# The integers of a quantized hidden layer: which are made beside the attention, where their ring of buffers lies, and which engine scales them

## The chip, the cores and the metric

The kernel runs on one core of one Trainium2 chip. The metric is the device time in microseconds of the whole program on that core; a number is the median of several executions. Beside it there is one profiled execution, whose trace gives every instruction's start and duration on each engine: TensorE (PE, matrix multiplication), VectorE (DVE), ScalarE (ACT), GpSimd (POOL), and SyncE (SP), which here only issues transfers. Transfers between the device memory (HBM) and the on-chip memory (SBUF) run on the core's 16 DMA engines, whichever engine issues them.

## The reference, cut to what matters

Two "Flamingo" layers work on x of shape (2, 2048, 512), 4096 rows of 512. Each layer is a gated cross attention to 128 context rows, then a gated feed-forward part. Everything up to the second layer's cross attention is the same before and after the change. The second feed-forward part is the place of the change:

```
x = x + tanh(g_xattn[1]) * xattn(layernorm(x), ctx)          # 16 heads of 64
h = bit_linear(layernorm(x), w1)                             # 512 -> 2048
h = silu(depthwise_conv1d(h) over the 2048 rows of a batch)  # three taps
x = x + tanh(g_ffn[1]) * bit_linear(h, w2)                   # 2048 -> 512
bit_linear(x, w): act_quant(x) times weight_quant(w)
act_quant(x): scale = 127 / max|x| of the row;  round(x * scale) / scale
weight_quant(w): scale = 1 / mean|w|;  clip(round(w * scale), -1, 1) / scale
```

The scale of a row of h is known only when all 2048 hidden values of that row have been computed. Then every value is multiplied by its row's scale and rounded to an integer, and the integers, which fit bf16 exactly, are multiplied with the ternary w2.

## The kernel before, in words

**Blocks.** Rows go in 8 blocks of 512 (4 for each batch). A block's hidden layer is held transposed: hidden units on the 128 partitions, 16 chunks (`HC`) of 128 units, 512 rows along the free dimension. So a block's hidden layer is 128 x 16 x 512, 4 MB in f32 and 2 MB as bf16 integers.

**Beside the attention (lines 213 to 328 and 1022 to 1124).** `cross_attention` runs 128 units, 16 for each block, plus 12 that let the pipeline run out. After a block's output projection (`back`, L315), `stage3_done` stores the block's rows to `x3_d` and queues two generators in `stream`: `quantize_rows` (layer norm and integers of the rows) and `first_half` (the matmuls L1002 with w1, the convolution L1012 to L1018, silu L1043, a store of the f32 hidden layer to `h_d` at L1049, the absolute maximum L1050 to L1056). When a block's first half is over, `scales_of` (queued in `ending`) makes its rows' scales (L1073, `hid_s`). After each unit, `beside4` moves these generators on.

For the first `EARLY` blocks (4 of them) a third list, `later`, holds `integers(g)`: chunk by chunk it loads `h_d` (L1094, `hf`, two buffers), multiplies by the scale on DVE (L1101), rounds (even chunks on DVE, L1107; odd ones with two ACT instructions, L1104 and L1105) and stores the bf16 integers to `hq_d` (L1108). `beside4` moves `later` on by one chunk in three of four units.

**The second half (from line 1271).** For each of the 8 blocks in turn, four row tiles (`down_and_out`): 16 matmuls each (L1232) of the block's integers `hq` with w2, then DVE adds the result to the row tile (L1235) and SP stores it (L1236). Row tiles are loaded from `x3_d` one block ahead (`row_tile`, L1162), into a ring of 8 (`x5`), the first ones into a ring of two (`x5w`). A ninth group of 32 matmuls (`ql`) does the last row of each batch. The integers come from `quantize_hidden(g)`, one block ahead: for `g < EARLY` it only loads `hq_d` (L1198); for the others it loads the f32 hidden layer in 8 pieces of two chunks (L1188, issued by ACT, `h5`), multiplies by the scale (L1207: three pieces of four on DVE, the fourth on POOL), and rounds (even pieces on DVE, L1215; odd ones with two ACT instructions, L1212 and L1213). The last block's hidden layer stays in SBUF. Blocks 6 and 7 finish their first halves inside this second half, beside the matmuls of blocks 0 to 3.

**Where buffers lie.** Pool `w5` takes the memory of the attention's working tiles, which is free as soon as the last unit is done (`second_half_starts`). Pool `act5` takes the memory of the attention's weights, which is free only after the last output projection. Before the change, even blocks' integers lie in `w5` (8 tiles) and odd blocks' in `act5` (8 tiles), and the `h5` pieces lie in both (2 and 4).

**Order.** Each engine's instruction order is fixed when the program is built: a scheduler in the framework merges the generators' instructions into one order for each engine, and each engine executes its own in that order, waiting on semaphores. Transfers take one of eight semaphores in turn, SP's and ACT's together, and the build makes each transfer wait until the one eight before it has landed.

Of the kernel before, what the change touches and what calls it, by code (L numbers as in the profile page):

```python
# [10 lines left out]
F32 = mybir.dt.float32  # L11
BF16 = mybir.dt.bfloat16
# [5 lines left out]
P = 128  # L18
B, S, D = 2, 2048, 512
NT = B * S // P  # L20
TPB = S // P
BLK = 512
TB = BLK // P
NBLK = S // BLK
# [8 lines left out]
HC = HID // P  # L33
# [10 lines left out]
def flamingo_kernel(ctx: ExitStack, tc: tile.TileContext, a: dict, out: bass.AP):  # L44
    nc = tc.nc
# [4 lines left out]
    def psum_pool(stack, name, bufs):  # L50
        return stack.enter_context(tc.tile_pool(name=name, bufs=bufs, space=PSUM))
# [875 lines left out]
    hid_f = const.tile([P, NT], F32, name="hid_f")  # L927
    h_d = [dramp.tile([P, HC, BLK], F32, name=f"h_d{g}") for g in range(B * NBLK)]
    LAST = B * NBLK - 1
    EARLY = 4  # L930
    hq_d = [dramp.tile([P, HC, BLK], BF16, name=f"hq_d{g}") for g in range(EARLY)]
    x3_d = [dramp.tile([S, D], F32, name=f"x3_d{b}") for b in range(B)]

# [61 lines left out]
    carry, ending, kept, act5 = {}, [], [], []  # L995
# [71 lines left out]
    def scales_of(g, amax):  # L1067
# [9 lines left out]
        nc.vector.tensor_scalar(hid_f[:, ts(g, TB)], inv, finstep, None, ALU.mult)  # L1077
        if g < EARLY:
            later.append(integers(g))

    def scales_spread(g):

        pb = ps_mm.tile([P, BLK], F32, name="pb5", tag="mm")
        bcast_rows(pb, hid_s[:, ts(g, TB)], ident)
        s_b = act4.tile([P, BLK], F32, name="s_b", tag="s_b", bufs=1)
        nc.scalar.copy(s_b, pb)
        return s_b

    def integers(g):


        def load(c):
            h = act4.tile([P, BLK], F32, name="hf", tag="hf", bufs=2)
            nc.sync.dma_start(out=h, in_=h_d[g][:, c, :])  # L1094
            return h

        s_b, h = scales_spread(g), load(0)
        for c in range(HC):
            behind = load(c + 1) if c + 1 < HC else None
            yield  # L1100
            nc.vector.tensor_tensor(h, h, s_b, ALU.mult)  # L1101
            q = act4.tile([P, BLK], BF16, name="hi", tag="hi", bufs=2)
            if c % 2:
                nc.scalar.activation(h, h, AF.Copy, bias=RND)  # L1104
                nc.scalar.activation(q, h, AF.Copy, bias=-RND)  # L1105
            else:
                nc.vector.tensor_scalar(q, h, RND, RND, ALU.add, ALU.subtract)  # L1107
            nc.sync.dma_start(out=hq_d[g][:, c, :], in_=q)  # L1108
            h = behind

    stream, later = [], []

    def advance(q):
        while q and next(q[0], q) is q:
            q.pop(0)

    def beside4(u, share=2):


        for _ in range(share):  # L1120
            advance(ending)
            advance(stream)
        if u is None or u % 4 != 1:
            advance(later)

    def stage3_done(n, tiles):
        for i, t in enumerate(tiles):
# [20 lines left out]


    w5, ps_5, quantizing, ahead = [], [], [], []  # L1150
    GQ, hq, used = 2, {}, []

    def row_tile(g, i):

        t = w5[0].tile([P, D], F32, name="x5w", tag="x5w", bufs=2)
        if g + i > 1:
            t = act5[0].tile([P, D], F32, name="x5", tag="x5", bufs=8)
        r, p = g % NBLK * BLK + i * P - 1, 0
        if r < 0:
            nc.sync.dma_start(out=t[0:1, :], in_=x3_d[g // NBLK][0:1, :])  # L1160
            r, p = 0, 1
        nc.sync.dma_start(out=t[p:, :], in_=x3_d[g // NBLK][ds(r, P - p), :])  # L1162
        return t, r, p

    def second_half_starts():
        units.close()
        w5.append(s4.enter_context(tc.tile_pool(name="w5", bufs=1)))
        w5.append(w5[0].tile([P, HC, D], BF16, name="w2q"))
        quantizing.append(quantize_hidden(0))
        nc.sync.dma_start(out=w5[1], in_=w2_d)  # L1170
        ps_5.append(psum_pool(s4, "s5_o", 4))
        next(quantizing[0], None)
        ahead.extend(row_tile(0, i) for i in range(2))

    def quantize_hidden(g):

        NK = HC // GQ
        hq[g] = []

        def load(k):  # L1180
            if g == LAST:
                return kept[k * GQ // GC][:, ds(k * GQ % GC, GQ), :]
            pool = (act5 if len(used) % 3 else w5)[0]
            used.append(g)
            h = pool.tile(
                [P, GQ, BLK], F32, name="h5", tag="h5", bufs=4 if pool is act5[0] else 2
            )
            nc.scalar.dma_start(out=h, in_=h_d[g][:, ts(k, GQ), :])  # L1188
            return h

        def integer_tile():
            pool = act5[0] if g % 2 else w5[0]
            hq[g].append(pool.tile([P, GQ, BLK], BF16, name="hq", tag="hq", bufs=NK))
            return hq[g][-1]

        if g < EARLY:
            for k in range(NK):
                nc.sync.dma_start(out=integer_tile(), in_=hq_d[g][:, ts(k, GQ), :])  # L1198
            return
        AHEAD = 4  # L1200
        hs = [load(k) for k in range(AHEAD)]
        s_b = scales_spread(g)
        yield
        for k in range(NK):
            h = hs.pop(0)
            eng = nc.gpsimd if k % 4 == 3 else nc.vector
            eng.tensor_tensor(  # L1207
                h, h, s_b.unsqueeze(1).to_broadcast([P, GQ, BLK]), ALU.mult
            )
            q = integer_tile()  # L1210
            if k % 2:
                nc.scalar.activation(h, h, AF.Copy, bias=RND)  # L1212
                nc.scalar.activation(q, h, AF.Copy, bias=-RND)  # L1213
            else:
                nc.vector.tensor_scalar(q, h, RND, RND, ALU.add, ALU.subtract)  # L1215
            if k + AHEAD < NK:
                hs.append(load(k + AHEAD))
            yield
# [19 lines left out]
    def last_tokens():  # L1238

        h = act5[0].tile([P, B, HC], F32, name="hl", tag="hl")  # L1240
        nc.scalar.activation(h, z_last, AF.Silu)
        own = row4.tile([P, B], F32, name="ownl", tag="lm")
        nc.vector.tensor_reduce(own, h, AX.X, ALU.max, apply_absolute_value=True)
        pm = ps_mm.tile([P, B, P], F32, name="pml", tag="mm")
        for b in range(B):
            nc.tensor.transpose(pm[:, b, :], own[:, b : b + 1].to_broadcast([P, P]), ident)
        m = row4.tile([P, B], F32, name="ml", tag="lm")
        nc.vector.tensor_reduce(m, pm, AX.X, ALU.max)
        nc.vector.tensor_scalar(m, m, 1e-5, None, ALU.max)
        s = row4.tile([P, B], F32, name="sl", tag="ls")  # L1250
        nc.vector.reciprocal(s, m)
        nc.vector.tensor_scalar(s, s, 127.0, None, ALU.mult)
        fin = row4.tile([P, B], F32, name="fl", tag="lf")
        nc.vector.reciprocal(fin, s)
        nc.vector.tensor_scalar(fin, fin, finstep, None, ALU.mult)
        q = act5[0].tile([P, B, HC], BF16, name="ql", tag="ql")
        for b in range(B):
            nc.vector.tensor_scalar(h[:, b, :], h[:, b, :], s[:, b : b + 1], None, ALU.mult)
        nc.vector.tensor_scalar(q, h, RND, RND, ALU.add, ALU.subtract)
        for b in range(B):  # L1260
            t = act5[0].tile([P, D], F32, name="x5", tag="x5", bufs=8)[0:1, :]
            nc.sync.dma_start(out=t, in_=x3_d[b][S - 1 : S, :])
            down_and_out(
                lambda c: q[:, b, c : c + 1],
                fin[0:1, b : b + 1],
                1,
                t,
                out[(b + 1) * S - 1 : (b + 1) * S, :],
            )

    while later:
        advance(later)
    ahead.extend(row_tile(0, i) for i in range(2, TB))
    for g in range(LAST + 1):
        if g == LAST - 1:
            while stream or ending:
                beside4(None)
            last_tokens()
        behind = quantize_hidden(g + 1) if g < LAST else iter(())
        for i in range(TB):  # L1280
            t, r, p = ahead.pop(0)
            down_and_out(
                lambda c: hq[g][c // GQ][:, c % GQ, ts(i, P)],
                hid_f[:, g * TB + i : g * TB + i + 1],
                P,
                t,
                out[ds(g // NBLK * S + r, P - p), :],
                p,
            )
            if g < LAST:  # L1290
                ahead.append(row_tile(g + 1, i))
            for _ in range(3):
                next(behind, None)
                beside4(None, 1)
# [65 lines left out]
```

## Time and profile before

| what | value |
|---|---|
| median of 3 runs | 1894.57 us (1889.44 to 1899.59) |
| profiled execution, its own time | 1896.89 us |
| its span, first to last instruction | 1892.8 us |
| busy in the span: PE, DVE, ACT, POOL | 89%, 69%, 55%, 29% |
| second layer's attention, first to last unit's scores | from 863.8 us to 1635.6 us of the span |
| second half, from the w2 load to the end | 1653.8 us to 1892.8 us, 239.0 us |
| PE busy in these 239.0 us | 190.9 us |

The profiled execution is 2.3 us above the median and its time 4.1 us above its span, so a span of this profile is 1.8 us under the median. PE's busy time counts pipelined matmuls with modelled ends; its idle gaps are the surer reading.

### The profile page before, as it was taken

How to read it: one execution, taken by the hardware profiler on the slowest of the kernel's cores; microseconds unless marked ns; L12 is line 12 of the kernel's file. 1: busy time of each engine (PE TensorE's matmuls, PEld its weight loads, DVE VectorE, ACT ScalarE, POOL GpSimd, SP SyncE). 2: the span in 40 equal slices, each digit the busy share in tenths (PEclk: the TensorE clock that was granted, in tenths of full speed). 3: DMA queues.
4: the chain of work that ended last, by engine and by line, in shares of the span. 5: the costliest groups of instructions: out<-in, count | busy, mean ns of one | idle time of the engine just before them, and what ended most of it. 6: DMA issues, size and time to landing. Idle time of an engine off the chain costs nothing.

```text
span 1892.8 us, 24174 instructions
## 1 busy us (share of the span) xinstructions
PE 1684.2 (89%) x7580; PEld 841.7 (44%) x7626; DVE 1312.3 (69%) x2713; ACT 1041.1 (55%) x3021; POOL 554.0 (29%) x676
## 2 busy tenths in 40 slices
PE   6989988888837989989999999999999999887877
PEld 4544544444313543445544444445444444433433
DVE  5777898878772432224447789799798789675956
ACT  1645545355402635205547778788787779643523
POOL 4534343343202310032214242323234233221212
PEclk9999999899958989999999999999999999898989
DMA  7011011011122019330011134234243133157463
GB/s 281 1 45 46 1 46 45 12 45 46 45 94 100 1 62 347 110 89 23 29 40 62 78 117 142 98 123 150 75 143 101 78 103 131 36 210 239 154 220 127
DMA packets 94998, 184.33 MB, mean 97 GB/s; under 512 B 10944, under 2 KB 30144, under 8 KB 91159
## 3 DMA queue, kind: packets, MB, share of 16 engines
q1 hardware_dynamic: 90518, 168.11, 25.5%
q10 hardware_dynamic: 3456, 12.58, 2.0%
q0 software_dynamic: 896, 2.10, 0.6%
q8 instruction: 60, 0.98, 0.2%
q14 instruction: 68, 0.55, 0.1%
HBM read 108.31 MB, written 74.45 MB: 97 GB/s over the span
## 4 chain that ended last, share of the span: by engine, by line
PE 37%; DVE 12%; DMA 6%; ACT 4%; issue 2%; POOL 2%; SPq 1%; ACTq 0%; DVEq 0%; POOLq 0%
PE pp L315 9%; PE pq L248 8%; PE ph L1002 3%; PE po L297 3%; PE sc L271 3%; DVE h L1018 2%; PE pu L875 2%; PE tp L289 2%; PE po L1232 2%; PE acc L861 2%; PE pw L875 2%; DMA h<-h_d 1%; DVE h L1207 1%; DMA out_x<-x 1%; DMA out_x<-x5w 1%
## 5 line engine op out<-in xcount | busy, mean ns | idle before, releaser
L128 POOL TENSOR_TENSOR A<-A,rden 128x512 f32<-128x512 f32 x280 | 298.2, 1067 | 552.4 <-DVE rden L127 448.6
L119 ACT ACTIVATE A<-sc,nmx 128x128 f32<-128x128 f32 x1024 | 362.8, 377 | 168.5 <-DVE nmx L116 145.8
L315 PE MATMUL pp<-L_wo,OT 128*128 128x512 f32 x768 | 366.1, 611 | 10.2 <-DVE x L324 6.8
L248 PE MATMUL pq<-xnT,L_wq 128*128 128x512 f32 x768 | 360.6, 616 | 0.0
L119 ACT ACTIVATION_READ_ACCUMULATOR A<-sc,nmx 128x1 f32 x1024 | 221.4, 216 | 0.0
L248 PEld LDWEIGHTS pq<-xnT,L_wq 128*128 128x128 f32 x768 | 146.1, 197 | 161.2 <-issue 153.3
L116 DVE TENSOR_REDUCE nmx<-sc 128x4 f32<-128x512 f32 x256 | 169.1, 677 | 67.1 <-PE sc L271 66.8
L290 DVE COPY AT<-tp 128x512 f32<-128x512 f32 x256 | 172.9, 677 | 56.5 <-PE tp L289 56.0
L315 PEld LDWEIGHTS pp<-L_wo,OT 128*128 128x128 f32 x768 | 138.9, 195 | 157.8 <-issue 135.1
L1018 DVE SCALAR_TENSOR_TENSOR h<-u,cw,h 128x512 f32<-128x512 f32 x256 | 190.7, 779 | 6.0 <-ACT h L1014 5.5
L289 PE MATMUL tp<-ident,A 128*128 128x128 f32 x1024 | 164.5, 283 | 28.3 <-POOL A L128 26.7
L271 PE MATMUL sc<-L_kT,qT 32*128 32x128 f32 (+1 forms) x2048 | 163.5, 290 | 5.8 <-ACT A L119 5.1
L271 PEld LDWEIGHTS sc<-L_kT,qT 32*128 32x128 f32 (+1 forms) x2048 | 130.4, 188 | 85.5 <-issue 60.8
L289 PEld LDWEIGHTS tp<-ident,A 128*128 128x128 f32 x1024 | 119.7, 143 | 103.0 <-issue 47.5
L1232 PE MATMUL po<-w2q,hq 128*128 128x512 bf16 x501 | 125.9, 406 | 37.6 <-DMA hq<-hq_d 12.8
L1014 ACT ACTIVATE h<-u,cb,cw 128x512 f32<-128x512 f32 x128 | 99.1, 809 | 59.3 <-DVE u L1012 52.3
L1002 PE MATMUL ph<-xiT,w1q 128*128 128x512 bf16 x477 | 122.4, 380 | 6.0 <-DVE u L1012 3.9
L297 PE MATMUL po<-AT,L_v 128*32 128x512 f32 (+1 forms) x512 | 118.8, 634 | 9.4 <-DVE AT L290 9.0
L305 ACT COPY OT<-po 128x512 f32<-128x512 f32 x96 | 55.8, 588 | 103.2 <-PE po L297 102.7
L1012 DVE TENSOR_TENSOR u<-ph,inv_b 128x512 f32<-128x512 f32 x128 | 85.0, 682 | 33.0 <-PE ph L1002 26.1
L1011 POOL COPY u<-carry 128x2 f32<-128x2 f32 x128 | 49.1, 386 | 200.1 <-DVE h L1018 171.7
L1232 PEld LDWEIGHTS <-hq 128*128 128x128 bf16 x512 | 51.2, 103 | 108.9 <-issue 23.4
(218 smaller groups left out, 2266.3 us busy)
## 6 DMA issues: line engine op xcount, KB each, us to landing
h_d<-h SPq DMA_DIRECT2D x28, 1024.0 KB, 4.1
x_d<-x SPq DMA_DIRECT2D x64, 256.0 KB, 2.0
hf<-h_d SPq DMA_DIRECT2D x64, 256.0 KB, 3.0
x<-x_d SPq DMA_DIRECT2D x60, 256.0 KB, 5.1
h<-h_d ACTq DMA_DIRECT2D x24, 512.0 KB, 6.0
x<-in_x SPq DMA_DIRECT2D x32, 256.0 KB, 5.4
xn_d<-xn SPq DMA_DIRECT2D x32, 256.0 KB, 2.2
xf<-x_d SPq DMA_DIRECT2D x32, 256.0 KB, 3.0
```

The source lines that it names most:

```text
L116: nc.vector.tensor_reduce(nmx, sc, AX.X, ALU.max, negate=True)
L119: nc.scalar.activation(out_tile[:, h, :], sc[:, h, :], AF.Exp, bias=nmx[:, h : h + 1], accum_out=den[:, h : h + 1],)
L128: nc.gpsimd.tensor_tensor(out_tile, out_tile, rden.unsqueeze(2).to_broadcast([P, n, width]), ALU.mult,)
L248: nc.tensor.matmul(pq, W.wq[:, d, ts(e, P)], xnT[:, d, :], start=(d == 0), stop=(d == DC - 1),)
L271: nc.tensor.matmul(sc[h][:, t, :], qT[e % cpg][r, ts(t, P)], W.kT[r, b, e, :], start=True, stop=True,)
L289: nc.tensor.transpose(tp[:, t, :], A[:, t, :], ident)
L290: nc.vector.tensor_copy(AT, tp.rearrange("p t n -> p (t n)"))
L297: nc.tensor.matmul(po[h * dh : (h + 1) * dh, :], W.v[:, b, ts(hd, dh)], AT[c * hpc + h], start=True, stop=True,)
L315: nc.tensor.matmul(pp, OT[e][:, ts(i, P)], W.wo[:, e, :], start=(e == 0), stop=(e == nE - 1),)
L1002: nc.tensor.matmul(ph, w1q[:, d, ts(c, P)], xiT[g][:, d, :], start=(d == 0), stop=(d == DC - 1),)
L1018: nc.vector.scalar_tensor_tensor(z, u[:, ds(k, BLK)], cw[:, c, k : k + 1], z, ALU.mult, ALU.add)
L1232: nc.tensor.matmul(po, rows(c), w2q[:, c, :], start=(c == 0), stop=(c == HC - 1))
```

## The change

Five edits, all for the second half's integers:

- `EARLY` goes from 4 to 5: block 4's integers are made beside the attention too, stored, and loaded as integers. `beside4` moves `later` on after every unit, not in three of four.
- The integer tiles form one ring of 16 in order of use: 12 in `w5`, 4 in `act5`. The loads of blocks 0 and 1 are now both started in `second_half_starts`, block 1's as far as its first four tiles.
- The f32 pieces `h5` all lie in `act5`, six of them.
- The multiplication by the scale is on DVE for every piece (L1205 after the change); POOL has none.
- Block 1's first row tile uses the ring of 8, not the ring of two (the test `g + i > 1` becomes `g * TB + i > 1`).

```diff
-    EARLY = 4
+    EARLY = 5
...
-        if u is None or u % 4 != 1:
-            advance(later)
+        advance(later)
...
-    GQ, hq, used = 2, {}, []
+    GQ, hq = 2, {}
+    next_integers = iter(range(B * NBLK * HC // GQ))
...
-        if g + i > 1:
+        if g * TB + i > 1:
             t = act5[0].tile([P, D], F32, name="x5", tag="x5", bufs=8)
...
-        quantizing.append(quantize_hidden(0))
         nc.sync.dma_start(out=w5[1], in_=w2_d)
         ps_5.append(psum_pool(s4, "s5_o", 4))
-        next(quantizing[0], None)
+        quantizing.extend(quantize_hidden(g) for g in range(2))
+        for q in quantizing:
+            next(q, None)
...
-            pool = (act5 if len(used) % 3 else w5)[0]
-            used.append(g)
-            h = pool.tile(
-                [P, GQ, BLK], F32, name="h5", tag="h5", bufs=4 if pool is act5[0] else 2
-            )
+            h = act5[0].tile([P, GQ, BLK], F32, name="h5", tag="h5", bufs=6)
...
         def integer_tile():
-            pool = act5[0] if g % 2 else w5[0]
-            hq[g].append(pool.tile([P, GQ, BLK], BF16, name="hq", tag="hq", bufs=NK))
+
+            pool, bufs = (w5[0], 12) if next(next_integers) % 16 < 12 else (act5[0], 4)
+            hq[g].append(pool.tile([P, GQ, BLK], BF16, name="hq", tag="hq", bufs=bufs))
...
             for k in range(NK):
+                if g == 1 and k == NK // 2:
+                    yield
                 nc.sync.dma_start(out=integer_tile(), in_=hq_d[g][:, ts(k, GQ), :])
...
-            eng = nc.gpsimd if k % 4 == 3 else nc.vector
-            eng.tensor_tensor(
+            nc.vector.tensor_tensor(
...
-        behind = quantize_hidden(g + 1) if g < LAST else iter(())
+        behind = quantizing[1] if g == 0 else quantize_hidden(g + 1) if g < LAST else iter(())
```

## The prediction, made before the changed kernel ran

> **What bounds the kernel now.** I read the page first (PE busy 89% of the span), then busy times by stage, then PE's timeline where it idles, then the waits behind those gaps. Busy times, one line for each of five attention blocks (by their first unit), then three stretches of the second half:
>
> ```profile
> core 0: us, PE busy (x) PEld busy (x) DVE busy (x) ACT busy (x) POOL busy (x), PEclk, DMA share, GB/s
> 1006.60:1112.70 106.10, 103.45 (x457) 51.30 (x460) 84.80 (x156) 81.09 (x198) 34.63 (x54) 1.00 0.25 90
> 1112.70:1220.60 107.90, 102.15 (x458) 50.65 (x462) 92.43 (x176) 85.82 (x208) 37.82 (x57) 0.98 0.33 113
> 1220.60:1325.80 105.20, 103.34 (x463) 51.45 (x469) 95.64 (x177) 88.24 (x211) 34.63 (x53) 1.00 0.38 131
> 1325.80:1432.70 106.90, 103.91 (x445) 50.14 (x448) 91.96 (x173) 84.93 (x204) 34.36 (x53) 0.98 0.33 115
> 1432.70:1537.60 104.90, 100.85 (x457) 50.46 (x461) 86.90 (x158) 83.60 (x204) 34.31 (x54) 1.00 0.26 91
> ...
> 1653.80:1702.00 48.20, 42.80 (x115) 18.11 (x118) 36.95 (x58) 24.88 (x22) 11.69 (x28) 0.93 0.53 202
> 1702.00:1789.10 87.10, 72.85 (x331) 32.02 (x336) 61.63 (x108) 36.84 (x39) 12.47 (x30) 0.92 0.58 196
> 1789.10:1893.00 103.90, 75.23 (x304) 31.22 (x310) 65.10 (x74) 34.85 (x36) 23.61 (x8) 0.86 0.52 177
> ```
>
> In the attention PE is 96% busy and a block takes 105 to 108 us. The first of the five has few integer chunks (they begin at 1094 us), the next three about 12, DVE's busy time goes from 85 to 96 us, and the length does not follow. In the second half PE idles: 14 us between 1702 and 1789, 29 after. PE's timeline, with the wait before each stretch in brackets:
>
> ```profile
> 1724.37 2.29 PE L1232 MATMUL po<-w2q,hq 128*128 128x512 bf16 x5 [9.70 <-DMA hq<-hq_d]
> ...
> 1770.71 17.86 PE L1232 MATMUL po<-w2q,hq 128*128 128x512 bf16 x80
> 1789.08 0.66 PE L1073 MATMUL pm<-ident,amax 128*128 128x128 f32 x4 [0.51 <-DVE amax L1056]
> ...
> 1796.06 9.51 PE L1232 MATMUL po<-w2q,hq 128*128 128x512 bf16 x36 [4.67 <-DVE hq L1215]
> ...
> 1818.12 3.59 PE L1232 MATMUL po<-w2q,hq 128*128 128x512 bf16 x8 [5.42 <-DVE hq L1215]
> 1827.71 6.64 PE L1232 MATMUL po<-w2q,hq 128*128 128x512 bf16 x18 [6.00 <-ACT hq L1213]
> ```
>
> First gap: block 1's integers are late. SP holds their loads behind a third use of the two-deep row ring, which waits for a store:
>
> ```profile
> SPq L1162 <- DMA out_x<-x5w: 7.5, 1, 7.5
> ```
>
> Later gaps: block 4 onwards must be scaled and rounded just ahead of the matmuls. One name's instructions (minimum/median/maximum ns):
>
> ```profile
> L1207 DVE TENSOR_TENSOR h<-h,s_b x24: 1187/1214/3376, 1790.8 to 1876.6; 128x1024 f32<-128x1024 f32 x24
> L1215 DVE TENSOR_SCALAR hq<-h x16: 673/681/2854, 1795.3 to 1878.4; 128x1024 bf16<-128x1024 f32 x16
> L1207 POOL TENSOR_TENSOR h<-h,s_b x8: 2361/2968/3393, 1790.9 to 1866.8; 128x1024 f32<-128x1024 f32 x8
> ```
>
> **What the Trainium skill says.** GPSIMD Engine Reference, Specifications: GpSimd shares its SBUF interfaces with VectorE where a VectorE instruction has two SBUF inputs. The trace agrees: the 24 DVE multiplications take 34.8 us, not 24 x 1.214 = 29.1, with maxima where POOL multiplies. PSUM — Partial Sum Buffer, Engine vs sequencer instructions: ScalarE's queue is strict FIFO; here ACT roundings stand 8.05 us behind a load that ACT itself must issue, which waits for a store. TensorE: Matmul & The Clock Gate, What's actually happening: an idle window lowers PE's clock, sustained work restores it; the granted clock is 1.00 in the attention, 0.86 after 1789.
>
> **The change, part by part.** The sum is against the profiled execution (span 1892.8); a span is 1.8 us under the median of the runs.
>
> *Attention.* 16 more chunks: DVE 16 x 0.76 + 8 x 0.48 = 16 us, ACT 8 x (0.63 + 0.63) = 10 us, SP 16 loads and 16 stores, 6 MB. The pace goes from 12 to 16 chunks a block, which five blocks of integers fill to about where four end now (about 1606 us). Cover: DVE idles 10 to 21 us a block, PE sets the length. Without cover it costs 16 us, and DVE's waits for `hf` loads (17.4 us on 64 chunks) would grow by 4. But about 17 us of each block (layer norm and row maxima, 1197 to 1214) are a DVE chain, where 4 more chunks of 1 us, a sixth of them exposed, make 0.7 us a block. I take +3, bounds 0 and +20; below nothing is excluded, no work leaves this stage.
>
> *1653.8 to 1702.* SP gains four integer loads (1 MB) and ACT loses two f32 pieces (1 MB) ahead of the h_d stores: 0.
>
> *1702 to the end, PE's account.* Before: 187.0 us to the last matmul, of which the timeline's gaps are 38.1 (13.8 to 1789.1, 24.3 after) and 148.9 busy. At the cadence of the stretch of 80 above (17.86/80 = 0.223), 536 + 64 matmuls take 134 us, transposes some 6: 140. So 9 us go to the lower clock. After:
>
> - Work: 140, plus 7 matmuls that the build's new order moves here from before 1702: 141.6.
> - First gap: 12.8 of the 13.8 us (all the waits for `hq` loads). Half of block 1's integers lie in memory that is free early and the row ring's third use is gone, so this goes. The other half is loaded near 1707 to 1710, lands (5.5 us) by 1716, when block 0 is done (64 x 0.223 from 1702).
> - A new wait: block 6's last h_d store stands on SP behind the first out_x store, which takes the semaphore of an f32 load that ACT issues at 1702 (6 us to land). Out at 1709, landed (8.5 us) at 1717.5, then ACT's Abs (1.9) and DVE's maxima (2.5) free PE's transpose at 1722, which it reaches at 1718. I take 4; bounds 0 and 6. ACT's row rounding for block 7 stands behind the same Abs.
> - Block 4 needs no scaling: 4.67 and part of 5.42 go. Its tiles are whole in the new order, where they were cut to pieces of two to four.
> - POOL's part: DVE takes all 24 multiplications, 29.1 us, and 12 roundings of 0.68, 8.2 us. It had 34.8 + 14.2 = 49.0. So no DVE time is added. For one block DVE needs 8 x 1.21 + 4 x 0.68 + 4 x 0.74 = 15.4 us, PE 64 x 0.223 = 14.3. With t0 when block 5's scale is ready, PE has three tiles of block 4 to do, to t0 + 11; the last of block 5's integers come from ACT at t0 + 17, PE can do much of block 5 by then. Wait: 2.
> - What is late next: block 6's last f32 pieces. ACT's seventh load uses the semaphore of a row-tile load, whose buffer waits for block 4's last store: DVE's add at t0 + 14, store landed (3.5) t0 + 18, row landed (6.1) t0 + 24.5, piece landed (6.0) t0 + 30.5, the eighth near t0 + 33. DVE's chain for `ql` stands behind it, ready at t0 + 36; PE has finished block 5 near t0 + 27.5 and has `ql` next. Wait: 9; bounds 0 (the loads were early) and 15.
> - Small gaps 1.5; lower clock after two waits 4.
>
> 141.6 + 4 + 2 + 9 + 1.5 + 4 = 162, against 187.0: -25. With the attention's +3, -22; after the last matmul 3.9 us stay. I shade this by -2, since the wait of 9 is a chain of worst cases: -24. Median 1894.6 - 24 = 1870, span 1869.
>
> **Rivals.** (a) No new wait: the loads are ahead and the clock stays up. Then 162 - 4 - 9 - 2 = 147 and the attention costs nothing: about 1856. For it: 177 GB/s after 1789 leaves room. Against: f32 loads and stores share semaphores. Chance 0.25.
> (b) Starvation stays: DVE now carries every multiplication and pieces still arrive late (POOL waited 54.0 us for them). The tail keeps its 24 us of gaps and its clock; only the first gap and block 4's work go: about -12, 1883. For it: 15.4 us of DVE a block is over PE's 14.3. Chance 0.15.
> (c) Slower: exposed `hf` loads. Every unit now has a chunk; DVE executes in order, so a late `hf` stops the attention's row maxima and transposes' copies behind it, and PE after them. Before, 17.4 us on 64 chunks, 0.27 each; with 80 chunks it would have to be 0.7 each, on PE's path, to eat 24 us and the 9.5 of the measurement: then 1905 and more. Against: a load lands in 3.0 us, a unit is 6.6. Chance 0.06.
> (The change not doing what it says is excluded by the build: its order has the early loads and POOL without multiplications.)
>
> **How the numbers follow.** My forecast has 0.54, own range 1862 to 1880; (a) 0.25, (b) 0.15, (c) 0.06. Predicted 1870. Range 1853 to 1888: (a) with its bounds below, (b) with a dearer attention above; it leaves out (c) and the ends. About 0.5%, 9.5 us, is what a measurement of this kernel can tell. Faster by more (under 1885.1): nearly all of the forecast and (a), over half of (b): 0.86. Same: 0.08. Slower: 0.06.
>
> **What would show it.** Blocks of the attention between 105 and 110 us with DVE near 96 to 100. No wait for `hq` loads of 9 us near 1715; a wait for `amax` of some 4 us instead. Block 4's 64 matmuls unbroken. DVE multiplications all near 1.21 us. A wait ahead of `ql` with the f32 load behind it. The prediction fails if the attention's blocks grow by over 4 us each, or if PE's gaps after the last first half still sum to over 20 us.

## The result

The kernel after takes 1899.36 us (median of 10 runs, 1895.72 to 1904.91), the kernel before 1892.85 us (1885.64 to 1899.59, 10 runs in the same session): ratio 1.0041, 95% interval 1.0022 to 1.0060. The forecast was 1870; the change costs 6.5 us instead of saving 24. That is less than the 0.5% that the prediction counted as a difference, but the interval lies above 1.

The profiled spans are 1903.2 and 1892.8 us, 10.4 apart (both from executions that took 4 to 6 us longer than their medians), and the difference splits in three. In the kernel after, the first unit of block 2 starts 5.9 us later (1012.4 against 1006.6; a unit's start is taken from VectorE's first row maximum for it), with the same code ahead of it. In the kernels below, which share that code too, this start lies anywhere between 1000.6 and 1013.6 us, so it is variation of a run. Blocks 2 to 6 of the attention take 540.5 us against 531.1: **+9.4**. From there to the end it is 350.3 us against 355.2: **-4.9**, where the forecast had -25 for the second half. Busy times by stage in the kernel after: the five attention blocks, then the second half from the w2 load in three stretches.

```profile
core 0: us, PE busy (x) PEld busy (x) DVE busy (x) ACT busy (x) POOL busy (x), PEclk, DMA share, GB/s
1012.40:1118.60 106.20, 103.52 (x457) 51.31 (x461) 84.64 (x155) 81.23 (x198) 34.51 (x54) 1.00 0.25 90
1118.60:1224.80 106.20, 103.42 (x453) 51.84 (x456) 94.63 (x174) 86.01 (x208) 35.34 (x53) 1.00 0.37 126
1224.80:1334.70 109.90, 105.88 (x458) 52.82 (x461) 97.01 (x177) 87.81 (x213) 37.03 (x55) 1.00 0.37 125
1334.70:1444.90 110.20, 106.01 (x462) 52.64 (x465) 100.98 (x185) 89.42 (x216) 38.48 (x56) 1.00 0.38 128
1444.90:1552.90 108.00, 105.05 (x465) 52.25 (x468) 95.75 (x174) 88.66 (x213) 37.55 (x54) 1.00 0.35 119
...
1667.70:1702.90 35.20, 30.64 (x93) 13.33 (x94) 27.31 (x43) 18.91 (x18) 9.58 (x23) 0.99 0.63 239
1702.90:1789.10 86.20, 70.18 (x294) 31.93 (x301) 56.46 (x98) 35.91 (x38) 12.26 (x33) 0.88 0.63 209
1789.10:1903.20 114.10, 82.16 (x359) 36.57 (x364) 65.46 (x95) 33.45 (x34) 1.06 (x2) 0.88 0.44 146
```

The last three blocks sit at the upper end of the forecast's 105 to 110 us. After 1702.9 PE idles 16 and 32 us. Behind the last first half (its maxima reach PE at 1807.6) it still waits 25.7 us; over 20 us there was the prediction's own sign that it fails. PE's timeline, after, where it waited longest (the wait and its releaser in brackets):

```profile
1743.75 1.11 PE L1073 MATMUL pm<-ident,amax 128*128 128x128 f32 x4 [15.12 <-DVE amax L1056]
...
1807.15 0.60 PE L1230 MATMUL po<-w2q,hq 128*128 128x512 bf16 x2 [2.09 <-DMA hq<-hq_d]
...
1838.27 12.04 PE L1230 MATMUL po<-w2q,hq 128*128 128x512 bf16 x45 [13.28 <-ACT hq L1211]
...
1863.04 8.57 PE L1230 MATMUL po<-w2q,ql 128*1 128x512 bf16 x32 [12.07 <-DVE ql L1257]
```

The wait of 9.7 us for block 1's integers is gone and block 4 needs no scaling, as said. In their place stand three long waits, of 15.1, 13.3 and 12.1 us, where the forecast had 4, 2 and 9. What was late shows in the chain of waits (start, duration, what), first ahead of 1743.75, then ahead of 1838.27:

```profile
1718.72 19.74 DMA h_d<-h
1738.46 0.02 issue
1738.48 0.02 ACTq L1050
...
1816.94 16.79 DMA out_x<-x
1833.73 0.02 issue
1833.75 0.32 SPq L1161
```

A store of the f32 hidden layer took 19.74 us, and a store of one row tile 16.79. The page's list of transfers has the median from issue to landing of such h_d stores (KB each, us). They are four times the size of a row tile, and over the whole kernel their median is 3.8 us.

```profile
h_d<-h SPq DMA_DIRECT2D x28, 1024.0 KB, 3.8
```

The store of 16.79 us is block 4's first row tile. The first tile of each batch has no row above it, so its store (and its main load) covers 127 partitions, not 128. The other long one, the h_d store, was issued on SP at 1718.72, right behind block 0's 127-row store of 1717.25, and SP needed 8.47 us to issue it:

```profile
1718.72 8.47 SPq L1049 DMA_DIRECT2D h_d<-h  x1
```

The kernel before has such a 127-row store too. Its own chain of waits has the line

```profile
1705.78 17.84 DMA out_x<-x5w
```

and this is the store for which its row ring waited. In the stretch of the kernel after in which that store of 1816.94 is alone, the 16 DMA engines are busy to 0.06, one sixteenth (columns as above):

```profile
1825.00:1834.00 9.00, 0.00 (x0) 0.00 (x0) 0.00 (x0) 0.00 (x0) 0.00 (x0) 0.70 0.06 24
```

The Trainium skill states why: DMA: Bandwidth & Descriptors, section "Why a DMA increments its semaphore by 16 and not by 1", says that a transfer issued by SP or ACT runs on the largest number of engines up to 16 that divides its outermost dimension, and names 127 partitions as a case of one engine. Its section "Queues, rings and completion order" says that each engine takes its descriptors in ring order. From this it follows that a later store of the same queue, one that uses all engines, stands behind the long store on that one engine.

This case's trace agrees. It records completion marks for each transfer: 16 for a store of a full tile, and for a 127-row store only one besides the mark at its issue. The h_d store of 1718.72 has 15 of its marks by 1731.9 and the last at 1738.5, 2.4 us behind the late mark of the 127-row store ahead of it (1736.0). The forecast had not used that page.

### The profile page after: what moved, and what is told of

Read it like the earlier page. It is cut to its first block, busy times and chain, and to the rows that moved or that the text cites. A ratio compares the mean times of both kernels' runs of the same rounds, so it can differ in the third digit from the quotient of the medians.

```text
span 1903.2 us, 24239 instructions
## 1 busy us (share of the span) xinstructions
PE 1690.5 (89%) x7582; PEld 851.3 (45%) x7626; DVE 1322.2 (69%) x2733; ACT 1041.9 (55%) x3029; POOL 535.2 (28%) x668
## 4 chain that ended last, share of the span: by engine, by line
PE 34%; DVE 15%; DMA 7%; ACT 3%; issue 2%; POOL 2%; SPq 0%; ACTq 0%; DVEq 0%; POOLq 0%
PE pq L248 7%; PE pp L315 7%; PE po L1230 3%; DVE h L1018 3%; PE ph L1002 3%; DMA h_d<-h 3%; PE po L297 2%; PE pu L875 2%; PE sc L271 2%; PE tp L289 2%; PE acc L861 2%; PE pw L875 2%; DVE u L1012 1%; DVE hf L1101 1%; DMA out_x<-x 1%
## 5 line engine op out<-in xcount | busy, mean ns | idle before, releaser
L289 PE MATMUL tp<-ident,A 128*128 128x128 f32 x1024 | 165.8, 283 | 27.0 <-POOL A L128 24.8
L1018 DVE SCALAR_TENSOR_TENSOR h<-u,cw,h 128x512 f32<-128x512 f32 x256 | 186.6, 765 | 2.6 <-ACT h L1014 2.1
L271 PE MATMUL sc<-L_kT,qT 32*128 32x128 f32 (+1 forms) x2048 | 175.9, 294 | 10.4 <-ACT A L119 7.8
L271 PEld LDWEIGHTS sc<-L_kT,qT 32*128 32x128 f32 (+1 forms) x2048 | 139.7, 190 | 92.3 <-issue 63.2
L1230 PE MATMUL po<-w2q,hq 128*128 128x512 bf16 x499 | 116.5, 389 | 16.3 <-ACT hq L1211 13.3
L311 POOL TENSOR_TENSOR x<-x,L_bo 128x512 f32<-128x512 f32 x64 | 88.3, 1398 | 35.6 <-DMA x<-x_d 12.9
```

What stands on the lines that cost most here:

```text
L271: nc.tensor.matmul(sc[h][:, t, :], qT[e % cpg][r, ts(t, P)], W.kT[r, b, e, :], start=True, stop=True,)
L289: nc.tensor.transpose(tp[:, t, :], A[:, t, :], ident)
L1018: nc.vector.scalar_tensor_tensor(z, u[:, ds(k, BLK)], cw[:, c, k : k + 1], z, ALU.mult, ALU.add)
L1230: nc.tensor.matmul(po, rows(c), w2q[:, c, :], start=(c == 0), stop=(c == HC - 1))
```

## Experiments

### The 127-row stores

To take the long stores away without moving anything, the first store of a batch is cut to 112 rows, which 16 divides. The order on every engine and on SP's queue stays as it was. (Rows 112 to 126 of each batch are not stored.)

```
-        nc.sync.dma_start(out=to, in_=t[p:, :])
+        if p:
+            nc.sync.dma_start(out=to[0:112, :], in_=t[1:113, :])
+        else:
+            nc.sync.dma_start(out=to, in_=t[p:, :])
```

> The kernel after, but the first row tile of each batch stores 112 of its 127 rows (rows 112 to 126 of each batch's output are left out); the order of every engine is otherwise the same, instruction by instruction. Theory A (a 127-row store occupies one DMA engine for some 17 us, and what stands behind it on the queue or on its semaphore waits): these two stores land in 4 to 6 us, PE's waits of 15.1 us (amax) and 13.3 us (hq) fall under 4 us each, the wait for ql shrinks, and the time is 1865 to 1878. Theory B (general crowding of DMA, or the number of rows does not matter): the waits stay, 1894 to 1902. Theory C (DVE is the bound of the last blocks, the stores only hide it): the amax wait goes, the others are replaced by waits for DVE, 1884 to 1890.

> The kernel before with the same edit (112 of 127 rows stored, rows 112 to 126 of each batch left out, order the same). Theory A: the first store no longer takes 17.8 us, so the row ring's third use does not wait and PE's gap of 9.7 us for block 1's integers shrinks to under 4; block 4's store, hidden or not, adds a little: 1878 to 1886. Theory B: 1889 to 1896.

> The kernel after with only block 0's first store cut to 112 rows (rows 112 to 126 of the first batch left out). Theory A: the amax wait of 15.1 us goes under 4, the hq wait of 13 us near 1838 and its store of 17 us stay: 1882 to 1890. Theory B: no change, 1894 to 1902.

> The kernel after with only block 4's first store cut to 112 rows (rows 112 to 126 of the second batch left out). Theory A: the amax wait of 15 us stays, the hq wait of 13.3 us goes under 4 and that for ql shrinks from 12: 1876 to 1888. Theory B: no change, 1894 to 1902.

| kernel | us | ratio to before, 95% interval |
|---|---|---|
| after, 112 rows | 1877.87 | 0.9932 (0.9908 to 0.9957) |
| before, 112 rows | 1873.97 | 0.9904 (0.9874 to 0.9934) |
| after, block 0's store only | 1891.76 | 1.0002 (0.9983 to 1.0021) |
| after, block 4's store only | 1889.41 | 0.9988 (0.9972 to 1.0004) |

The 15 rows cost the kernel after 21.5 us (1899.36 - 1877.87) and the kernel before 18.9 (1892.85 - 1873.97). PE's timeline of the kernel after with 112 rows, all waits over 0.4 us after 1702:

```profile
1723.03 1.11 PE L1073 MATMUL pm<-ident,amax 128*128 128x128 f32 x4 [4.60 <-DVE amax L1056]
1786.67 0.61 PE L1230 MATMUL po<-w2q,hq 128*128 128x512 bf16 x2 [1.28 <-DMA hq<-hq_d]
1801.20 1.04 PE L1230 MATMUL po<-w2q,hq 128*128 128x512 bf16 x4 [1.39 <-ACT hq L1211]
1806.39 11.79 PE L1230 MATMUL po<-w2q,hq 128*128 128x512 bf16 x46 [2.00 <-ACT hq L1211]
1833.24 9.05 PE L1230 MATMUL po<-w2q,ql 128*1 128x512 bf16 x32 [14.40 <-DVE ql L1260]
```

The waits of 15.1 and 13.3 us are now 4.6 and 2.0. With block 0's store alone cut, the first is 4.9 and the second 13.5; with block 4's alone, 14.3 and 3.0: each store makes the wait that was put down to it. The two kernels with one store cut end 1 to 2 us above what theory A expected, the kernel before with 112 rows 4 us below it, and ql's wait did not shrink, it grew to 14.4. The h_d store behind block 0's is issued in 0.32 us and lands in 9.3 us in place of 19.7 (112 rows, SP's timeline and the list of transfers):

```profile
1708.42 0.32 SPq L1049 DMA_DIRECT2D h_d<-h  x1
...
h_d<-h SPq DMA_DIRECT2D x1, 1024.0 KB, 9.3
```

So the long store cost this one 10.4 us. Why it takes 9.3 us here and 3.8 in the median was not tried.

In the kernel before, the same edit turns the wait of 9.7 us for block 1's integers into 1.4 and 1.6. So that gap was the work of block 0's 127-row store from the start. The wait of 6.0 us at 1827.71, which the prediction shows behind a rounding of ScalarE's, is gone with the edit too. That rounding waited 8.05 us behind a load that itself waited for a store, and in the trace of before this store, issued at 1816.70, has 15 marks by 1819.5 and its last at 1826.1, behind block 4's 127-row store (1824.9).

The price by itself, from a chain of transfers at the end of the kernel before, each waiting for the one ahead of it, a store (L1299) and the load back (L1300) for every row count:

```
+    for f, n in ((0, 128), (0, 128), (1, 127), (0, 127), (0, 126), (0, 125), (0, 120), (0, 112), (0, 96), (0, 64), (0, 15), (0, 128)):
+        nc.sync.dma_start(out=scr[0:n, :], in_=tm[f : f + n, :])
+        nc.sync.dma_start(out=tm[f : f + n, :], in_=scr[0:n, :])
```

> The kernel before with a chain of transfers added at its end, each waiting for the one ahead of it: a tile of 128 partitions by 512 f32 stored to DRAM and loaded back, with 128, 128, 127 (from partition 1), 127 (from partition 0), 126, 125, 120, 112, 96, 64, 15 and 128 rows. Theory A (rows are dealt to DMA engines in equal parts, so a count that has few divisors falls on one engine): a store of 127 rows 12 to 18 us from either partition, 112 and 128 under 4, 126 and 125 and 120 in between by their divisors. Theory B (only the partition offset of 1 matters): the 127 rows from partition 0 land in under 5 us. Theory C (the 17 us were queueing): all under 5 us.

SP's timeline of that kernel (start, us to issue; a transfer's time is the distance to the next start), from the second 127-row store to the 125-row pair:

```profile
1914.40 0.22 SPq L1299 DMA_DIRECT2D scr<-x  x1
1926.94 0.22 SPq L1300 DMA_DIRECT2D x<-scr  x1
1939.24 0.31 SPq L1299 DMA_DIRECT2D scr<-x  x1
1941.68 0.31 SPq L1300 DMA_DIRECT2D x<-scr  x1
1944.37 0.25 SPq L1299 DMA_DIRECT2D scr<-x  x1
1948.28 0.25 SPq L1300 DMA_DIRECT2D x<-scr  x1
1952.32 0.32 SPq L1299 DMA_DIRECT2D scr<-x  x1
```

127 rows: stored in 12.5 us, loaded in 12.3; from partition 1 it was 12.8 and 12.3. 126 rows: 2.4 and 2.7. 125: 3.9 and 4.0. 120 and 112: 2.4 and 2.3, stored. 128 (the last): 2.0. Theory A holds, and the divisors fit the page of the skill: 126 has 14, 125 only 5, 127 none but 1.

The loads of these tiles have 127 rows too, and they stay in every kernel here. None of PE's waits ends on one, but one ends on what stands behind it: block 4's, issued in the kernel after at 1793.91, has its late mark at 1806.5, and the integer load issued on SP at 1794.25 has 15 marks by 1799.9 and the last at 1807.1. This is PE's wait of 2.09 us above. What the kernels would gain without these loads was not tried.

### What the change is worth without the long stores, and a whole output

The two 112-row kernels say what the change itself does: 1877.87 against 1873.97, +3.9 us, though with four runs each their two intervals overlap. The profiles have the attention at 541.7 us for the five blocks against 531.8 (+9.9) and the rest at 329.6 against 334.4 (-4.8). To have the output whole, the store is split:

```
+            nc.sync.dma_start(out=to[0:112, :], in_=t[1:113, :])
+            nc.sync.dma_start(out=to[112:127, :], in_=t[113:P, :])
```

and in a third kernel, besides, block 4's integers are left out of the attention again, with the rest of the change kept:

```
-    EARLY = 5
+    EARLY = 4
...
-        advance(later)
+        if u is None or u % 4 != 1:
+            advance(later)
```

> The kernel after with the first row tile of each batch stored in two transfers, 112 rows and 15, so that the output is whole. The additional transfer moves the build's order of the second half a little. If the 127-row store is the cause, 1873 to 1884 (1877.9 with 112 rows alone); if the additional transfer or the changed order costs what the store cost, 1890 or more.

> The kernel before with the same split in two transfers, 112 rows and 15. If the 127-row store is the cause, 1870 to 1880 (1874.0 with 112 rows alone); otherwise 1888 or more. The change's own worth, with the long store out of both kernels, is then s_after against s_before: +2 to +6 us.

> The kernel after with the split store, and with block 4's integers left out of the attention (EARLY 4, no chunk on every fourth unit). By the sum of the parts 1866 to 1873, below both kernels with the split; if the changed order takes that away, 1875 to 1882.

> The 112-row form of the kernel after (rows 112 to 126 of each batch left out) with block 4's integers taken out of the attention again: EARLY back to 4 and no integer chunk on every fourth unit, all else as after. Theory A (the fifth block's chunks cost the attention 9 to 10 us and are worth about 5 to 7 in the second half): attention blocks 2 to 6 together 530 to 534 us against 541.7, time 1871 to 1877 against 1877.9. Theory B (they are worth more than they cost): 1880 or more.

Split stores: after 1885.56 us (ratio to before 0.9961, 0.9944 to 0.9979), before 1875.26 (0.9890, 0.9862 to 0.9917), after with EARLY at 4 1870.24 (0.9869, 0.9844 to 0.9894). With 112 rows, EARLY at 4 is 1868.61 (0.9865, 0.9819 to 0.9910), five blocks 532.9. So the split repairs both kernels, before almost wholly and after by two thirds; after ends above its expectation, and so does the change's worth with the split, +10.3 us where 2 to 6 were expected. PE waits 16.1 us for ql in it. VectorE's and ScalarE's orders are the same as in the kernel after, and on SP one load besides the two new stores changes its place; what keeps the last third is not shown. The last kernel is ahead of both kernels of this case, by some 22 us of before; its lead over the repaired kernel before is within the two intervals.

Block 4's integers beside the attention are the part of the change that loses: 9.3 us with 112 rows (1877.87 - 1868.61, intervals that just touch) and 15.3 us with the split (1885.56 - 1870.24, intervals clear of each other). They do not shorten the second half either: from the end of the output projection to the last matmul it takes 163.6 us with EARLY at 4 and 167.1 with 5 (112 rows).

### The wait for ql

The two last tokens' part is emitted one block later, so that PE has it behind block 6.

```
                 beside4(None)
-            last_tokens()
+        if g == LAST:
+            last_tokens()
```

> The 112-row form of the kernel after, with the two last tokens' part emitted one block later, so that PE has them behind block 6 and not ahead of it. Theory A (the wait of 14.4 us ahead of ql comes from VectorE's ql chain standing behind block 6's pieces, whose f32 loads stand behind row-tile loads that wait for stores): the wait shrinks to waits of at most 6 us for block 6's integers, 1866 to 1873. Theory B (block 6's integers come just as late): waits for hq take its place, 1875 to 1879.

1870.82 us (0.9865, 0.9817 to 0.9913), 7 us under its base, with intervals that just touch. PE waits once for block 6's integers, 6.7 us, in place of 14.4 for ql. Theory A, a little over its 6.

### The attention

All kernels here have 112 rows; "five" is from the first unit of block 2 to that of block 7, in the one profile of each kernel. How far such a number moves from run to run shows in kernels that share the attention's code: the six profiles with 80 chunks (the kernel after and its forms above) lie between 539.2 and 541.7 us, the six with 64 (the kernel before and its forms, and EARLY at 4) between 531.1 and 535.2.

> The 112-row form of the kernel before (rows 112 to 126 of each batch left out) with an integer chunk on every unit, so 16 a block for the same 64 chunks of four blocks. Theory A (a pace of 16 a block costs 3 to 4 us in each block that has it): blocks 3 to 5 at 109 to 111, block 6 as before, 541 to 545 for five, time 1881 to 1888. Theory B (what costs is the number of chunks): five blocks at 530 to 534, time 1872 to 1877.

> The 112-row form of the kernel after, with the same 16 integer chunks a block, but none on units with u mod 4 = 1 and two on units with u mod 4 = 3. Theory A (the chunk's place costs: the unit after the first of four has other VectorE work): attention blocks 2 to 6 together 530 to 536 us, time 1868 to 1874. Theory B (the 16 us of VectorE work cost wherever they stand): blocks 540 to 545, time 1876 to 1882.

> The 112-row form of the kernel after (rows 112 to 126 of each batch left out), with every second integer chunk of the attention multiplied straight into its bf16 tile, without VectorE's rounding (these integers are left unrounded): VectorE has 8 x 0.42 = 3.4 us a block less. Theory A (the attention's growth of 9 to 10 us is VectorE's additional work): blocks 2 to 6 together fall from 541.7 to 530 to 537 us. Theory B (ScalarE's work or the transfers): 540 to 543.

> The 112-row form of the kernel after, with the other chunks multiplied straight into bf16, without ScalarE's two rounding passes (left unrounded): ScalarE has 8 x 1.26 = 10 us a block less, VectorE the same. Theory A (VectorE): blocks 2 to 6 together stay at 539 to 543 us. Theory B (ScalarE): 530 to 536.

> The 112-row form of the kernel after, with the multiplication of every second chunk on GpSimd: VectorE has 8 x 0.68 = 5.4 us a block less, if GpSimd does not hold it up. Theory A (VectorE's work lengthens the blocks): 530 to 537 us for five blocks, time 1868 to 1874. If GpSimd's work holds VectorE up or comes late for the rounding, 540 to 548, time 1877 to 1884.

> The 112-row form of the kernel after, with all computing taken out of the attention's integer chunks: each chunk's load stays, its store writes a tile of zeros (the integers of blocks 0 to 4 are left out), and VectorE and ScalarE do nothing for it. If the chunks' computing on the two engines together lengthens the blocks: five blocks at 528 to 534 us, against 541.7. If the transfers, or their instructions on SP, do it: 538 to 543.

> The 112-row form of the kernel after, with the chunk loads of the attention taken out (one load a block; every chunk computes from it, so that the integers of blocks 0 to 4 are wrong in all but the first chunk) and computing and stores kept. If computing lengthens the blocks: five blocks at 538 to 544 us. If the loads, or VectorE's waits for them, do it: 529 to 535.

The edits, in this order: `beside4` advances `later` after every unit in the kernel before; then, all on the kernel after,

```
-        advance(later)
+        for _ in range(1 if u is None else (1, 0, 1, 2)[u % 4]):
+            advance(later)
...
-                nc.vector.tensor_scalar(q, h, RND, RND, ALU.add, ALU.subtract)
+                nc.vector.tensor_tensor(q, h, s_b, ALU.mult)
...
-                nc.scalar.activation(h, h, AF.Copy, bias=RND)
-                nc.scalar.activation(q, h, AF.Copy, bias=-RND)
+                nc.vector.tensor_tensor(q, h, s_b, ALU.mult)
...
-            nc.vector.tensor_tensor(h, h, s_b, ALU.mult)
+            (nc.vector if c % 2 else nc.gpsimd).tensor_tensor(h, h, s_b, ALU.mult)
...
-            q = act4.tile([P, BLK], BF16, name="hi", tag="hi", bufs=2)
+            q = zero[0]
...
-            behind = load(c + 1) if c + 1 < HC else None
```

| kernel | chunks | five, us | time, us |
|---|---|---|---|
| before | 64 | 531.8 | 1873.97 |
| after, EARLY 4 | 64 | 532.9 | 1868.61 |
| before, a chunk on every unit | 64 | 535.9 | 1873.03 |
| after | 80 | 541.7 | 1877.87 |
| after, none on u mod 4 = 1, two on 3 | 80 | 548.9 | 1886.84 |
| after, no rounding of even chunks (VectorE) | 80 | 539.8 | 1879.10 |
| after, no rounding of odd chunks (ScalarE) | 80 | 544.2 | 1881.86 |
| after, even chunks multiplied on GpSimd | 80 | 557.9 | 1898.96 |
| after, no computing in the chunks (two runs) | 80 | 525.2 | 1866.98 |
| after, no loads of the chunks | 80 | 544.7 | 1879.41 |

Busy times over the five blocks, 112-row kernel after, then the same without computing in the chunks:

```profile
1002.60:1544.30 541.70, 526.62 (x2309) 261.19 (x2308) 472.25 (x861) 432.94 (x1040) 178.95 (x269) 1.00 0.35 117
```

```profile
1012.90:1538.20 525.30, 507.89 (x2278) 253.86 (x2301) 400.97 (x757) 395.34 (x970) 174.10 (x270) 1.00 0.31 109
```

Of VectorE's 71 us and ScalarE's 38 us of chunk work, 16.5 us (541.7 - 525.2) reach the length of the blocks. With 64 chunks it is 7.7 us (532.9 - 525.2), so the 16 additional chunks cost 8.8 (in each kernel a few chunks lie past these five blocks). The computing does it, not the transfers: without the computing, loads and stores kept, the growth is gone, and without the loads the blocks stay long. VectorE's waits for chunk loads fell with the change, from 17.4 to 2.4 us (waits of the kernels before and after):

```profile
DVE hf L1101 <- DMA hf<-h_d: 17.4, 20, 2.1
```

```profile
DVE hf L1101 <- DMA hf<-h_d: 2.4, 6, 0.7
```

Which engine's part does it is not settled. Without VectorE's rounding the blocks take 539.8 us, inside the spread of unchanged kernels; without ScalarE's 544.2, 2.5 above it. So neither rounding alone explains the growth; the multiplication, or both engines together, is left. Each of these edits, and the two without computing and without loads, also makes the build place the chunks anew, which by itself can cost 7 us (the kernel with two on u mod 4 = 3, slower than both of its theories). A pace of a chunk on every unit, with 64 of them, lengthened two blocks to 110.2 and 111.7 us and gave part of it back in block 6 (102.6), and cost no time. On GpSimd, a chunk's multiplication took 1.27 us against VectorE's 0.68, and VectorE waited 24.9 us for it; this kernel too is slower than either of its theories.

In PE's account the growth looks like work: PE's busy time grows by 10 us (513.7 to 523.9). Grouped by line and shape over the five blocks, before and after, the same 642 score matmuls are busy for 7.6 us more at the same mean:

```profile
L271 PE MATMUL sc<-L_kT,qT 64*128 64x128 f32 x642 | 54.1, 289 | 0.0
```

```profile
L271 PE MATMUL sc<-L_kT,qT 64*128 64x128 f32 x642 | 61.7, 290 | 0.0
```

With the same mean and a longer union, they overlap less: they lie further apart and still count as busy. The share of 96% said that PE had no idle time, not that nothing on another engine set its pace.

## Why the prediction was wrong

The attention came out 6.4 us above its term, and the stage from the end of the output projection to the last matmul 24 us above its 162. Most of the second is one step.

**First gap.** The step that failed is "the row ring's third use is gone, so this goes", and with it the duration of the first row tile's store, which the sum left out. The ring's wait went; what made it, the 127-row store of 17.84 us, stayed. The prediction knew it as "7.5 us" of SP's wait and never asked for the store's own duration, which stands in the chain of waits of before.

**The new wait for amax.** Right in mechanism and place, wrong in size: "out at 1709, landed (8.5 us) at 1717.5" became 1718.72 plus 19.74 us. The store was behind block 0's long one in SP's queue, and no longer ahead of it: before, this h_d store was issued at 1701.45. 15.1 us against 4. With 112 rows the store lands in 9.3 us and the wait is 4.6: the 8.5 and the 4 were right for a queue without the long store.

**Block 5, "wait: 2".** 13.3 us, from block 4's 127-row store: SP's next row load waited for that store's buffer until 1833.75, the store behind this load went out at 1834.16, and ACT's next f32 load and rounding waited until these had landed. The prediction took "store landed (3.5)" from 128-row stores. With 112 rows, 2.0. It had named this chain, for block 4's last store and for `ql`.

**`ql`, 9 within 0 to 15.** 12.1, and 14.4 without the long stores. What it is behind was right: the trace's chain ahead of it has an f32 load (1854.73, 5.19 us) that ACT issued behind a rounding which waited for a store, and moving `ql` behind block 6 shortened the wait.

**Block 4 and POOL.** Nearly right: block 4's matmuls are broken once, by the 2.09 us for its last integers behind the 127-row load, and VectorE's part is as worked out (29.1 and 8.2 us forecast). Groups by line and shape, after, from 1700 us on:

```profile
L1205 DVE TENSOR_TENSOR h<-h,s_b 128x1024 f32<-128x1024 f32 x24 | 28.4, 1215 | 3.0 <-DMA h<-h_d 2.5 <-ACT s_b L1086 0.3
...
L1213 DVE TENSOR_SCALAR hq<-h 128x1024 bf16<-128x1024 f32 x12 | 8.2, 682 | 0.0
```

**The sum of the second half, -25.** The prediction's account runs from the end of the output projection to the last matmul. PE's timeline has both ends (start, us), two lines for each kernel: after, before, and these two with 112 rows.

```profile
1702.89 10.21 PE L315 MATMUL pp<-L_wo,OT 128*128 128x512 f32 x16 [4.46 <-DVE u L1012]
1871.77 27.57 PE L1230 MATMUL po<-w2q,hq 128*128 128x512 bf16 x125 [0.16 <-issue]
1693.53 8.56 PE L315 MATMUL pp<-L_wo,OT 128*128 128x512 f32 x16
1874.31 14.61 PE L1232 MATMUL po<-w2q,hq 128*128 128x512 bf16 x59 [0.35 <-DVE hq L1215]
1694.21 8.68 PE L315 MATMUL pp<-L_wo,OT 128*128 128x512 f32 x16 [4.64 <-DVE u L1012]
1842.22 27.80 PE L1230 MATMUL po<-w2q,hq 128*128 128x512 bf16 x128
1693.01 8.40 PE L315 MATMUL pp<-L_wo,OT 128*128 128x512 f32 x16
1852.43 14.81 PE L1232 MATMUL po<-w2q,hq 128*128 128x512 bf16 x60 [0.35 <-DVE hq L1215]
```

It takes 186.2 us after and 186.8 before, where 162 was forecast. PE's waits in it sum to 43.4 us against 16.5 forecast (4, 2, 9 and 1.5), so the waits are the miss; the rest is 142.8 us against 145.6 (141.6 and the clock's 4). With 112 rows it is 167.1 us after, with waits of 24.2, and 165.8 before. So the change by itself gains nothing in this stage, and the 19 to 21 us are the long stores', in either kernel. That the kernel after with 112 rows, at 329.6 us from block 7's first unit to the end, lies 25.6 under the 355.2 of before is a coincidence with the sum's 25. The 4.9 us that the kernel after did gain lie ahead of this stage, from block 7's first unit to the end of the output projection (160.2 against 164.5 us; the other profiles of unchanged code give 158.6 to 163.5 and 161.2 to 164.7). Their cause is not shown.

**Clock.** The granted clock after 1702.9 was 0.88 and 0.88, against 0.92 and 0.86. By the sum above the term "lower clock after two waits 4" was not too small.

**Attention, +3 within 0 to 20.** +9.4. Cover was taken from VectorE's idle time, 10 to 21 us a block, less a sixth of four chunks. 16 chunks cost 8.8 us, 0.55 each, where 64 cost 0.12 each.

**Rivals.** (c), 1905 and more, points the right way, but by a mechanism that did not occur: the waits for `hf` fell, and VectorE's and ScalarE's computing for the chunks lengthened the blocks. (a) and (b) both assumed that the first gap goes.

## What to carry to other kernels

Before a wait's removal is booked as a gain, look up how long the thing it waited for itself takes, and what that holds up next: a slow transfer that one buffer no longer waits for is still in the queue. Check the row count of every transfer for its largest divisor up to 16: here one row less than 128 cost ten us, two rows less next to nothing, and a split into 112 and 15 rows took most of it back. A long transfer also costs those behind it on the queue. Idle time of an engine that works in the order of a pipeline was cover for the first additional work here, and less so for the last: price the marginal piece by a block that already has the higher load.

## What the runs showed of the hardware that was not expected

A store of 127 rows of 2 KB takes 12.5 us by itself (about 21 GB/s) and 16.8 to 18.8 us in this kernel's traffic (1736.0 - 1717.25 the longest); of 126 rows, 2.4 us. A 1 MB store issued right behind it takes 19.7 us in place of 9.3, and SP 8.5 us to issue it in place of 0.3. Where such a store is alone, the 16 engines are busy to 0.06. That 40 multiplications of 128 x 512 moved from VectorE to GpSimd lengthen five attention blocks by 16.2 us was not expected either.
